# Layer 4 of a graph network: the 8-bit counts loaded nine pieces ahead, x and the own parts loaded through SP's queue

## The chip, the cores and the metric

The kernel runs on one core of a Trainium2 chip. The metric is the device time of one execution in microseconds; the time before is 2769.23 us, the median of three runs (2764.82 to 2772.06).

The engines are called as in the profile: PE (matrix products) with PEld (its weight loads), DVE (VectorE), ACT (ScalarE), POOL (GpSimd) and SP (SyncE, which only issues transfers). A transfer is issued by an engine, in that engine's order of instructions, so an instruction that waits holds back the transfers behind it.

## The reference

A graph of 6250 nodes with 256 features and 100000 edges (src to dst, sorted by dst) passes through four layers, and the result is added to x:

```python
h = jnp.maximum(_layernorm(x, axis=-1), 0.0)
h = _sage_mean(features, edge_src, edge_dst, n, deg, W1_self, W1_neigh, b1)
h = _sage_pool(h, edge_src, edge_dst, n, deg, W2_pool, b2_pool, W2_self, W2_neigh, b2)
h = _sage_gcn(h, edge_src, edge_dst, n, deg, W3_neigh, b3)
h = _sage_mean(h, edge_src, edge_dst, n, deg, W4_self, W4_neigh, b4)
return h @ W_fc + b_fc        # and x + this
```

Layer 4 is `h @ W_self + mean(h[src] over the edges of each node) @ W_neigh + b`. The kernel multiplies by the weights before it sums: what is left for the last stage is, for each node, the mean over its edges of rows of a table, plus an own part and x.

## The kernel before, in words

Nodes lie in 49 tiles of 128. Since dst is skewed to low numbers, a layer treats its first tiles (22 in layer 4, `H4`) as dense and the rest as sparse.

**Dense tiles.** `dense` (L569) forms, for one tile of targets, the sum over all 49 tiles of sources of a 128x128 matrix of edge counts times the sources' rows `zt` (128x512, the 256 features split into two halves): 22 x 49 = 1078 products into the PSUM bank `pd`. The counts are a table of 8-bit numbers in HBM (`tab_a`). `stream` (L1731) brings them: `load` (L1734) issues pieces of up to seven count tiles on ACT's queue (`nc.scalar`, L1742) into five buffers `ac`, four pieces ahead of the products; `widened` (L1750) turns a piece into 32-bit numbers `af` on ACT, three pieces ahead. Both are called at a piece's first product.

**Sparse tiles.** `sums` fetches 128 edges at a time: POOL gathers the rows of their sources into a ring of 14 slots (L495, 266 gathers in layer 4), DVE makes a one-hot matrix from the edges' targets (L491, six ahead), PE multiplies both into `pg` (L513), four gathers to a bank, and DVE adds `pg` to the sums `acc` (L545 the first, L547 the others). `Hub.advance` puts the dense products between the gathers, about four to each. The gathers, the products and the sums are issued in one order in the program; each engine then runs its own part of it in that order.

**Finishing a tile.** For each of the 49 tiles `load4` loads x into a buffer `xr4` (L1848) and the own part, left in HBM by layer 3, into `q4` (L1850); there are seven buffers of each, 128 KB each, and both loads are on ACT's queue. `finish4` adds the own part to x (L1864), then the sums times 1/degree (L1866; twice for a dense tile, once for each half of `pd`, as for the sparse `acc`), both on DVE, and stores the tile on SP's queue (L1869, called out). The instructions stand where the framework's scheduler puts them: it moves a load, and the addition at L1864, forward as soon as a buffer is free by its own reckoning. A load into an `xr4` buffer waits for the store of the tile that held it, a load into a `q4` buffer for DVE's L1864 of the tile that held it. Each transfer of SP and ACT counts up one of eight completion counters (DMAHW0 to 7), with one transfer under way on each.

**Source tiles.** 23 of the 49 tiles of `zt` are kept in SBUF from layer 3 (`z4_kept`, L1784); the other 26 (`z4_late`) are loaded from HBM at the start of layer 4 in four transfers on SP's queue (`resident`, L1774). The first 2 x 23 = 46 products use only kept tiles. Layer 4's first count pieces are loaded when its buffers open, at the start of layer 3 (about 1955 us), where ACT issues them; that layer's sums have a `stream` of their own (L1831).

Of the kernel before, what the change touches and what calls it, by code (L numbers as in the profile page):

```python
# [12 lines left out]
F8 = mybir.dt.float8e4  # L13
# [8 lines left out]
P = 128  # L22
# [57 lines left out]
def fast_path(  # L80
# [15 lines left out]
    nc = tc.nc  # L96
# [1631 lines left out]

    upto2.close()

    def stream(pool, chunks, wide_pool=None):  # L1731

        got = {}
        where = {(d, s): i for i, (d, s0, s1) in enumerate(chunks) for s in range(s0, s1)}  # L1734

        def load(i):
            if i >= len(chunks):
                return
            d, s0, s1 = chunks[i]
            got[i] = pool.tile([P, 7, P], F8, name="ac", bufs=5)  # L1740
            t = got[i][:, : s1 - s0, :]
            nc.scalar.dma_start(t.bitcast(BF16), tab_a[d, :, s0:s1, :])  # L1742

        wide = {}

        def widened(i):
            if i < len(chunks):
                n = chunks[i][2] - chunks[i][1]
                wide[i] = wide_pool.tile([P, 7, P], F32R, name="af", bufs=5)
                nc.scalar.copy(wide[i][:, :n, :], got[i][:, :n, :])  # L1750

        for i in range(4):
            load(i)
        if wide_pool:
            widened(0)
            widened(1)
            widened(2)

        def block(d, s):
            i = where[d, s]  # L1760
            if s == chunks[i][1]:
                if wide_pool:
                    widened(i + 3)
                load(i + 4)
            return (wide if wide_pool else got)[i][:, s - chunks[i][1], :]

        return block
# [10 lines left out]
    with ExitStack() as on:  # L1778
        psd = on.enter_context(tc.tile_pool(name="psd3", bufs=2, space=PSUM))
        psg = on.enter_context(tc.tile_pool(name="psg3", bufs=3, space=PSUM))  # L1780
        psm = on.enter_context(tc.tile_pool(name="psm3", bufs=2, space=PSUM))
        zk = on.enter_context(tc.tile_pool(name="fz4", bufs=1, side="right"))
        Z4 = {}
        z4_kept = ((20, 27), (27, 34), (34, 41), (41, 43))  # L1784
        z4_late = ((0, 7), (7, 14), (14, 20), (43, NT))
        for s0, s1 in z4_kept:
            zt = zk.tile([P, s1 - s0, 2 * FO], F32R, name=f"zt{s0}", bufs=1)
            Z4.update({s: zt[:, s - s0, :] for s in range(s0, s1)})

        with tc.tile_pool(name="fl3", bufs=2) as wk:  # L1790
            def done3(d, acc):
                q = wk.tile([P, FH], F32, name="q", bufs=2)
                if d < H3:
                    nc.vector.tensor_add(q, acc, acc3[d])
                    nc.vector.scalar_tensor_tensor(q, q, rgcn[:, d : d + 1], qrow,
                                                   op0=ALU.mult, op1=ALU.add)
                else:
                    if d in Z3:
                        z = Z3[d]
                    else:  # L1800
                        z = wk.tile([P, 3 * FH], BF16, name="zown", bufs=1)
                        with tc.issue_after(kept_stores[-1].ins):
                            nc.sync.dma_start(z, tab_r[d * P : (d + 1) * P, :])
                        yield 1
                        yield 1
                        yield 1
                    if d < NT - 4:
                        for part in range(3):
                            nc.vector.tensor_add(acc, acc, z[:, part * FH : (part + 1) * FH])
                            yield 1  # L1810
                    else:
                        own = bank(psm, "pm", "pm_own")
                        for part in range(3):
                            nc.tensor.matmul(own, ident_b, z[:, part * FH : (part + 1) * FH],
                                             start=(part == 0), stop=(part == 2))
                        yield 1
                        nc.vector.tensor_add(acc, acc, own)
                    nc.vector.scalar_tensor_tensor(q, acc, rgcn[:, d : d + 1], qrow,
                                                   op0=ALU.mult, op1=ALU.add)
                q2 = Z4[d] if d in Z4 else wk.tile([P, 2 * FO], F32R, name="q2")  # L1820
                halves(q[:, FO:], FO, q2)
                nc.sync.dma_start(tab_s[d * P : (d + 1) * P, :], q2.bitcast(F32))
                nc.sync.dma_start(xq[d * P : (d + 1) * P, :], q[:, :FO])
                yield 1

            late = ((0, 5), (5, KEPT), (EARLY[1], NT))
            Z3 = {s: kept_rows[:, s, :] for s in range(KEPT)}
            with tc.issue_after(kept_stores[-1].ins):
                for s0, s1 in late[2:]:
                    Z3.update(resident(wk, tab_r, FH, s0, s1))  # L1830
            block = stream(wk, [(d, s0, s1) for d in range(H3) for s0, s1 in late])  # L1831
            todo = []
            work = []
            for d in range(H3):
                work += dense([s for s0, s1 in late for s in range(s0, s1)], lambda s, d=d: block(d, s), lambda s: Z3[s], FH, psd,
                              lambda acc, d=d: todo.append(done3(d, acc)), own=d)
            sums(wk, psg, tab_r, FH, srcE, keyE, jb, H3, done3, 11, Hub(work), wait=14, todo=todo,
                 rest=12)

        upto3.close()  # L1840
        settle(zk, on.enter_context(tc.tile_pool(name="flp", bufs=1, space=PSUM)))
        with tc.tile_pool(name="fl4", bufs=2) as wk:
            loaded4 = {}

            def load4(d):
                n = P if d < NFULL else NREM
                xr = wk.tile([P, FI], F32, name="xr4", bufs=7)
                nc.scalar.dma_start(xr[:n, :], x[d * P : d * P + n, :])  # L1848
                q = wk.tile([P, FO], F32, name="q4", bufs=7)
                nc.scalar.dma_start(q[:n, :], xq[d * P : d * P + n, :])  # L1850
                loaded4[d] = n, xr, q

            def done4(d, acc):
                for i in (d, d + 1) if H4 <= d < NT - 1 else (d,):
                    if i not in loaded4:
                        load4(i)
                return finish4(d, acc)

            def finish4(d, acc):
                n, xr, q = loaded4.pop(d)  # L1860
                yield 1
                yield 1
                yield 1
                nc.vector.tensor_add(xr[:n, :], xr[:n, :], q[:n, :])  # L1864
                for c in range(0, acc.shape[1], FO):
                    nc.vector.scalar_tensor_tensor(xr[:n, :], acc[:n, c : c + FO],  # L1866
                                                   rmean[:n, d : d + 1], xr[:n, :],
                                                   op0=ALU.mult, op1=ALU.add)
                nc.sync.dma_start(out[d * P : d * P + n, :], xr[:n, :])  # L1869

            order = [*z4_kept, *z4_late]
            block = stream(zk, [(d, *c) for d in (0, 1) for c in z4_kept]
                           + [(d, *c) for d in (0, 1) for c in z4_late]
                           + [(d, *c) for d in range(2, H4) for c in order],
                           wk)
            todo = []
            parts4 = []
            for d in range(H4):
                parts4.append(dense([s for s0, s1 in order for s in range(s0, s1)],
                                    lambda s, d=d: block(d, s), lambda s: Z4[s], FO, psd,  # L1880
                                    lambda acc, d=d: todo.append(done4(d, acc)), wide=True))
            nk = sum(s1 - s0 for s0, s1 in z4_kept)
            hub = Hub([w for d in (0, 1) for w in parts4[d][:nk]]
                      + [w for d in (0, 1) for w in parts4[d][nk:]]
                      + [w for p in parts4[2:] for w in p])
            hub.advance(2 * nk)
            for s0, s1 in z4_late:
                Z4.update(resident(wk, tab_s, FO, s0, s1))
            sums(wk, psg, tab_s, FO, srcE, keyE, jb, H4, done4, 14, hub, wait=4, todo=todo,
                 rest=8, wide=True)  # L1890
# [643 lines left out]
```

## Time and profile before

| what | us |
| --- | --- |
| median of three runs | 2769.23 |
| the profiled execution, its own time | 2768.88 |
| its span, first to last instruction | 2767.1 |
| mean granted TensorE clock | 0.936 |
| layer 4's first product starts at | 2388.0 |
| last gather starts at | 2750.83 |

Over the whole span PE is busy 2363.3 us (85%), DVE 2074.8 (75%), POOL 1881.4 (68%) and ACT 1240.6 (45%). The page's share of busy time is an average over very different stages; what matters here is the last 380 us. A row of a group reads: line, engine, operation, output <- inputs, count | busy us, mean ns | idle time of the engine just before these, and what ended it. A row of the waits reads: engine, tile and line, what it waited for: us in total, times, the longest.

### The profile page before, as it was taken

The page shows a single profiled execution, that of the slowest core. Times are in us where ns is not written, and L with a number is a line of the kernel's source. Part 1 is how long each engine was busy: PE and PEld are TensorE (multiplying, and loading weights), DVE is VectorE, ACT ScalarE, POOL GpSimd, SP SyncE. Part 2 cuts the span into 40 slices and gives each one's busy share as a digit, 9 for nine tenths or more (in the row PEclk, how much of TensorE's full clock was granted, in tenths as well). Part 3 has the DMA queues.
Part 4 walks back from the last instruction along what each step waited for, and adds up shares of the span by engine and source line. Part 5 has one row for each costly group of instructions (what it writes and reads, how often), then busy time and mean ns, then how long its engine had stood idle before and what let it go on. Part 6 is the DMA issues. An engine that isn't in the chain of part 4 may idle for free.

```text
span 2767.1 us, 38367 instructions
## 1 busy us (share of the span) xinstructions
PE 2363.3 (85%) x10823; PEld 1341.6 (48%) x10913; DVE 2074.8 (75%) x5438; ACT 1240.6 (45%) x2833; POOL 1881.4 (68%) x2193
## 2 busy tenths in 40 slices
PE   3688999999686565788899998799899999798897
PEld 2356666767443222343344443344344444476676
DVE  8888777766699898788788897774376777466666
ACT  5467777763388887753444343211000000244333
POOL 5477777777566676777667776663477777577675
PEclk8799999999897687899999999999999999899999
DMA  8567777777799999999999999895799999999897
GB/s 273 154 183 204 208 210 212 223 228 222 243 362 334 309 351 318 331 347 345 315 307 331 342 357 298 296 311 189 280 370 382 379 391 388 328 344 308 284 302 225
DMA packets 360123, 815.18 MB, mean 295 GB/s; under 512 B 58798, under 2 KB 149014, under 8 KB 359868
## 3 DMA queue, kind: packets, MB, share of 16 engines
q0 software_dynamic: 145168, 511.30, 56.6%
q1 hardware_dynamic: 142248, 211.90, 21.1%
q10 hardware_dynamic: 72484, 89.43, 9.5%
q8 instruction: 89, 1.46, 0.2%
q14 instruction: 134, 1.10, 0.1%
HBM read 607.75 MB, written 205.46 MB: 294 GB/s over the span
## 4 chain that ended last, share of the span: by engine, by line
PE 45%; DMA 27%; DVE 14%; issue 5%; ACT 3%; POOL 2%; ACTq 0%; DVEq 0%; POOLq 0%
PE pd L575 14%; PE pg L516 11%; DMA X<-rows,srcIf 9%; DVE run L1631 5%; PE pd L569 4%; DMA ring<-tab_h,srcT 4%; DMA rows<-X 4%; PE pm_hp L1176 3%; DMA xr<-in_x 2%; DVE X L1631 2%; PE pm_prf L1548 2%; PE pm_hp L1170 2%; PE pb L346 2%; POOL X L1650 2%; DVE acc L547 1%
## 5 line engine op out<-in xcount | busy, mean ns | idle before, releaser
L1650 POOL DMA_INDIRECT X<-rows,srcIf x782 | 742.6, 950 | 346.6 <-issue 147.5
L1631 DVE SCALAR_TENSOR_TENSOR run<-run,samef,X 128x512 f32<-128x512 f32 x758 | 572.4, 755 | 65.3 <-DMA X<-rows,srcIf 59.6
L495 POOL DMA_INDIRECT ring<-tab_h,srcT x474 | 456.3, 963 | 148.9 <-issue 53.4
L516 PE MATMUL pg<-ring,hot 128*128 128x256 bf16 (+2 forms) x2342 | 492.1, 317 | 45.7 <-DMA ring<-tab_h,srcT 33.5
L575 PE MATMUL pd<-kept_rows,ae 128*128 128x512 bf16 x1520 | 395.0, 393 | 61.2 <-DVE acc L1307 48.2
L495 POOL DMA_INDIRECT ring<-tab_r,srcE x314 | 317.4, 1011 | 126.6 <-issue 49.4
L547 DVE SCALAR_TENSOR_TENSOR acc<-pg,M,acc 128x256 f32<-128x256 f32 (+2 forms) x629 | 322.8, 540 | 76.6 <-PE pg L516 72.5
L569 PE MATMUL pd<-zt,af 128*128 128x512 f32 x1078 | 305.8, 406 | 46.9 <-ACT af L1750 40.1
L516 PEld LDWEIGHTS <-hot 128*128 128x128 bf16 x2364 | 230.7, 98 | 233.2 <-issue 88.0
L495 POOL DMA_INDIRECT ring<-tab_s,srcE x266 | 254.4, 956 | 122.7 <-PE pg L513 48.7
L1631 DVE SCALAR_TENSOR_TENSOR X<-X,samef,run 128x512 f32<-128x512 f32 x379 | 282.2, 744 | 53.8 <-DMA X<-rows,srcIf 35.0
L575 PEld LDWEIGHTS <-ae 128*128 128x128 fp8e4 x1728 | 171.8, 100 | 305.3 <-issue 156.7
L569 PEld LDWEIGHTS pd<-zt,af 128*128 128x128 f32 x1078 | 208.0, 195 | 104.8 <-ACT af L1750 44.4
L1750 ACT CAST af<-ac 128x896 fp32r<-128x896 fp8e4 (+2 forms) x176 | 146.6, 846 | 217.5 <-PE pd L569 53.8
L491 DVE TENSOR_SCALAR hot<-iota_bf,keyE 128x128 bf16<-128x128 bf16 (+1 forms) x580 | 152.9, 284 | 107.8 <-PE pg L516 75.4
L1548 PE MATMUL pm_prf<-unf,hTf 128*128 128x512 f32 x384 | 197.4, 641 | 3.3 <-ACT hTf L1538 3.3
L401 ACT ACTIVATE A<-pb 128x392 fp8e4<-128x392 f32 x224 | 109.3, 499 | 191.2 <-PE pb L396 177.9
L338 ACT ACTIVATE hs<-ht,onef 128x128 bf16<-128x128 bf16 x396 | 153.5, 393 | 88.7 <-PE pb L346 87.7
L575 PE MATMUL pd<-Z,A 128*128 128x256 bf16 (+1 forms) x1176 | 184.6, 274 | 0.7 <-ACT A L351 0.6
L372 ACT ACTIVATE ht<-iota_bf,skR 128x128 bf16<-128x128 bf16 x448 | 155.9, 400 | 13.3 <-DMA col<-in_L_gnn_b 9.4
L337 ACT ACTIVATE ht<-iota_bf,sk 128x128 bf16<-128x128 bf16 x396 | 153.1, 398 | 8.3
L340 DVE TENSOR_SCALAR hm<-iota_w,mk 128x392 bf16<-128x392 f16 x461 | 150.5, 334 | 5.1 <-PE pb L346 4.8
(378 smaller groups left out, 3794.5 us busy)
## 6 DMA issues: line engine op xcount, KB each, us to landing
rows<-X SPq DMA_DIRECT2D x385, 256.0 KB
tab_r<-kept_rows ACTq DMA_DIRECT2D x44, 384.0 KB
ac<-tab_a ACTq DMA_DIRECT2D x128, 112.0 KB
rows<-hpf SPq DMA_DIRECT2D x49, 256.0 KB
th<-tab_t ACTq DMA_DIRECT2D x49, 256.0 KB
X<-rows,srcIf POOLq DMA_INDIRECT x782
tab_a<-A ACTq DMA_DIRECT2D x14, 784.0 KB
tab_t<-th SPq DMA_DIRECT2D x37, 256.0 KB
```

The lines of the kernel that those rows point to most:

```text
L337: nc.scalar.activation(t, iota_b, AF.Abs, bias=sk[:, r : r + 1])
L338: nc.scalar.activation(hots[0], t, AF.Relu, bias=one, scale=-1.0)
L372: nc.scalar.activation(held["ht"][:, i, :], iota_b, AF.Abs, bias=sk[:, r : r + 1])
L491: nc.vector.tensor_scalar(hot[j], iota_b, keyT[:, j - jb : j - jb + 1], None, op0=ALU.is_equal)
L495: nc.gpsimd.indirect_dma_start(out=ring[:, j % deep, :].bitcast(F32) if wide else ring[:, j % deep, :], out_offset=None, in_=table, in_off ...
L516: mm = nc.tensor.matmul(pg[:, : F + c], hot[j], X[:, part * F : (part + 1) * F + c], start=(k == 0 and part == 2), stop=(k == n - 1 and pa ...
L547: nc.vector.scalar_tensor_tensor(acc[d], half, m, acc[d], op0=ALU.mult, op1=ALU.add)
L569: nc.tensor.matmul(hold[0], a, z, start=(s == ss[0]), stop=(s == ss[-1]))
L575: nc.tensor.matmul(hold[0][:, : F + c], a, z[:, part * F : (part + 1) * F + c], start=(s == ss[0] and part == 2 and s != own), stop=(s == ...
L1548: nc.tensor.matmul(pm, hT[:, c, :], un[:, c, :], start=False, stop=(c == KH - 1))
L1631: nc.vector.scalar_tensor_tensor(put, held, st, row, op0=ALU.mult, op1=ALU.max)
L1650: nc.gpsimd.indirect_dma_start(out=X[:, k, :], out_offset=None, in_=tab_p, in_offset=bass.IndirectOffsetOnAxis(ap=srcI[:, t : t + 1], axis=0),
```

## The change

The stream of counts takes a parameter `deep` (4 unless given), and layer 4 gives 9: nine pieces are loaded ahead, in ten buffers instead of five. To make room, two source tiles less are kept (21), and 28 are loaded late, in five transfers; so the first products are 42. The loads of x and of the own parts go from ACT's queue to SP's. Layer 3's stream stays at four; the seven buffers of `xr4` and `q4` stay.

```diff
-    def stream(pool, chunks, wide_pool=None):
+    def stream(pool, chunks, wide_pool=None, deep=4):
...
-            got[i] = pool.tile([P, 7, P], F8, name="ac", bufs=5)
+            got[i] = pool.tile([P, 7, P], F8, name="ac", bufs=deep + 1)
...
-        for i in range(4):
+        for i in range(deep):
             load(i)
...
-                load(i + 4)
+                load(i + deep)
...
-        z4_kept = ((20, 27), (27, 34), (34, 41), (41, 43))
-        z4_late = ((0, 7), (7, 14), (14, 20), (43, NT))
+        z4_kept = ((22, 29), (29, 36), (36, 43))
+        z4_late = ((0, 7), (7, 14), (14, 18), (18, 22), (43, NT))
...
                 xr = wk.tile([P, FI], F32, name="xr4", bufs=7)
-                nc.scalar.dma_start(xr[:n, :], x[d * P : d * P + n, :])
+                nc.sync.dma_start(xr[:n, :], x[d * P : d * P + n, :])
                 q = wk.tile([P, FO], F32, name="q4", bufs=7)
-                nc.scalar.dma_start(q[:n, :], xq[d * P : d * P + n, :])
+                nc.sync.dma_start(q[:n, :], xq[d * P : d * P + n, :])
...
-                           wk)
+                           wk, deep=9)
```

The scheduler orders the instructions anew. ACT, in the second half of layer 4, has this before (casts are the widening; each load of x, of an own part and of counts in one line):

```order
L1742 DMA ac_26464<-tab_a_69 128x448 [waits DMAHW7_49,Activation_49]
L1848 DMA xr4_26760<-in_x 128x256 [waits DMAHW6_49,DMAHW0_49,DVE_49]
L1750 CAST af_26410<-ac_26393 128x768 [waits PE_49]
L1742 DMA ac_26478<-tab_a_69 128x128 [waits DMAHW2_49,Activation_49]
L1750 CAST af_26416<-ac_26412 128x768 [waits PE_49]
L1750 CAST af_26443<-ac_26418 128x896 [waits DMAHW3_49,PE_49]
L1742 DMA ac_26513<-tab_a_69 128x448 [waits Activation_49]
L1742 DMA ac_26532<-tab_a_69 128x448 [waits DMAHW4_49,Activation_49]
L1750 CAST af_26462<-ac_26445 128x896 [waits DMAHW5_49,PE_49]
L1848 DMA xr4_26835<-in_x 128x256 [waits DMAHW1_49,DVE_49]
L1742 DMA ac_26555<-tab_a_69 128x384 [waits Activation_49]
L1850 DMA q4_27305<-xq_70 128x256 [waits DMAHW7_49,DVE_49]
```

After the change only the casts and the count loads are left there. The loads of x and own parts stand on SP, between the stores, which were alone there before; around the same tiles (out_0 is the store):

```order
L1869 DMA out_0<-xr4_26349 128x256 [waits DMAHW3_49,DVE_49]
L1848 DMA xr4_26767<-in_x 128x256 [waits DMAHW6_49,DMAHW3_49]
L1869 DMA out_0<-xr4_26218 128x256 [waits DMAHW7_49,DVE_49]
L1850 DMA q4_27317<-xq_70 128x256 [waits DMAHW1_49,DVE_49]
L1848 DMA xr4_26848<-in_x 128x256 [waits DMAHW7_49,DMAHW2_49]
L1850 DMA q4_27346<-xq_70 128x256 [waits DMAHW5_49,DVE_49]
L1869 DMA out_0<-xr4_26381 128x256 [waits DVE_49]
L1848 DMA xr4_26930<-in_x 128x256 [waits DMAHW7_49,DMAHW3_49]
L1869 DMA out_0<-xr4_26519 128x256 [waits DMAHW4_49,DVE_49]
```

An x load there waits for the store in its buffer (the counter DMAHW7 of the second store, for xr4_26848) and holds the store after it; the own-part loads wait for DVE.

DVE, at the same tiles, before: the L1866 that finishes the tile in a buffer (xr4_26212) and, further down, the L1864 that reads the next x in that buffer (xr4_26835; a new number is a new tile in one of the seven buffers):

```order
L1866 SCALAR_TENSOR_TENSOR xr4_26212<-acc_26105,rmeanf_124,xr4_26212 128x256 [waits DVE_49]
...
L491 TENSOR_SCALAR hot_26502<-iota_bf_105,keyE_10813 128x128 [waits PE_49]
L491 TENSOR_SCALAR hot_26519<-iota_bf_105,keyE_10813 128x128 [waits PE_49]
...
L1866 SCALAR_TENSOR_TENSOR xr4_26375<-acc_26218,rmeanf_124,xr4_26375 128x256 [waits DVE_49]
...
L1866 SCALAR_TENSOR_TENSOR xr4_26506<-pd_26340,rmeanf_124,xr4_26506 128x256
L1864 TENSOR_TENSOR xr4_26835<-xr4_26835,q4_26837 128x256 [waits DMAHW5_49,DMAHW1_49]
L547 SCALAR_TENSOR_TENSOR acc_26381<-pg_26492,M_121,acc_26381 128x256 [waits PE_49]
```

And after the change, where the same buffer's tiles are called xr4_26218 and xr4_26848:

```order
L1866 SCALAR_TENSOR_TENSOR xr4_26218<-acc_26111,rmeanf_124,xr4_26218 128x256 [waits DVE_49]
...
L491 TENSOR_SCALAR hot_26513<-iota_bf_105,keyE_10813 128x128 [waits PE_49]
L1864 TENSOR_TENSOR xr4_26848<-xr4_26848,q4_26850 128x256 [waits DMAHW7_49,DMAHW2_49]
L491 TENSOR_SCALAR hot_26530<-iota_bf_105,keyE_10813 128x128 [waits PE_49]
...
L1866 SCALAR_TENSOR_TENSOR xr4_26381<-acc_26224,rmeanf_124,xr4_26381 128x256 [waits DVE_49]
```

Between the two rows that share a buffer stand 27 rows of DVE before and 14 after: the L1864 has moved up by 13.

## The prediction

> **What bounds the kernel now.** I read the windows of the last stage first, then its groups of instructions, its waits and the chain of waits. The change touches only layer 4 (2387 to 2767 us) and the loads that layer 3 starts ahead for it. The rows of the windows give, for each stretch, the busy time of each engine with its count of instructions, then the granted clock, the DMA share and the rate:
>
> ```profile
> 2412.00:2424.00 12.00, 4.58 (x11) 3.44 (x12) 0.91 (x3) 2.56 (x3) 2.48 (x3) 0.64 1.05 378
> 2430.00:2500.00 70.00, 69.48 (x303) 56.60 (x303) 46.55 (x143) 29.99 (x36) 53.07 (x56) 1.00 0.99 340
> 2500.00:2600.00 100.00, 90.31 (x380) 70.07 (x378) 63.98 (x200) 41.01 (x49) 75.25 (x79) 1.00 0.95 311
> 2600.00:2630.00 30.00, 23.80 (x86) 18.27 (x87) 15.98 (x50) 12.26 (x15) 16.69 (x18) 0.89 0.81 243
> 2630.00:2700.00 70.00, 65.63 (x274) 51.87 (x273) 41.05 (x130) 27.78 (x34) 50.68 (x53) 0.98 0.93 302
> 2700.00:2761.00 61.00, 52.15 (x216) 41.90 (x214) 44.06 (x131) 21.50 (x26) 34.40 (x36) 0.94 0.77 243
> ```
>
> From 2430 to 2500 POOL starts 56 gathers in 70 us, one each 1.25 us, and PE is busy throughout: this is the stage's best pace. Later it is missed. At 1.25 us each, the 79, 18, 53 and 36 gathers of the other rows would need 98.8, 22.5, 66.3 and 45.0 us; they had 100, 30, 70 and (the last gather starts at 2750.83) about 51. So about **18 to 20 us** are lost after 2500, and that is all this stage can win there. The groups and the waits say who loses it:
>
> ```profile
> L495 POOL DMA_INDIRECT ring<-tab_s,srcE x266 | 254.4, 956 | 122.7 <-PE pg L513 48.7 <-issue 33.5 <-PE pd L569 25.5
> L1864 DVE TENSOR_TENSOR xr<-xr,q 128x256 f32<-128x256 f32 (+1 forms) x49 | 20.7, 424 | 124.0 <-DMA xr<-in_x 99.1 <-DMA q<-xq 16.7 <-DMA ac<-tab_a 7.3
> ```
> ```profile
> DVE xr L1864 <- DMA xr<-in_x: 99.1, 27, 5.7
> PE pd L569 <- ACT af L1750: 25.9, 21, 5.1
> ACT af L1750 <- DMA ac<-tab_a: 22.3, 9, 4.2
> ACT af L1750 <- DMA xr<-in_x: 12.2, 3, 5.6
> DVE xr L1864 <- DMA q<-xq: 7.9, 5, 2.7
> ACT af L1750 <- DMA out<-xr: 7.6, 2, 7.2
> DVE xr L1864 <- DMA ac<-tab_a: 7.3, 1, 7.3
> ACT af L1750 <- DVE xr L1866: 7.1, 2, 5.1
> DVE acc L547 <- PE pg L513: 2.2, 4, 0.8
> DVE xr L1864 <- issue: 1.0, 1, 1.0
> DVE xr L1866 <- PE pd L569: 0.9, 1, 0.9
> ```
>
> The second fence holds the waits from 2430 on (total, times, longest). DVE waits 99.1 + 7.9 + 7.3 + 1.0 = **115.3 us** at one line, the addition of a tile's own part to its x (L1864), and only about 3 us for PE. The busy DVE times of the windows above add up to 212 us; 212 + 115 + 3 = 330 of the 331 us to 2761. DVE is thus always either at work or waiting for x. PE's 25.9 us behind ACT's widening are real, but beside a DVE that has no slack. The chain of waits from 2490 to 2720 shows why x is late (start, length, what):
>
> ```profile
> 2564.38 3.07 DMA out<-xr
> 2596.67 4.07 DMA out<-xr
> 2600.80 4.19 DMA xr<-in_x
> 2605.08 0.42 DVE xr L1864
> 2606.10 0.79 DVE acc L547 x2
> 2607.30 3.88 DMA out<-xr
> 2611.25 4.20 DMA xr<-in_x
> 2615.54 0.43 DVE xr L1864
> 2616.98 4.34 DMA out<-xr
> 2621.39 3.59 DMA xr<-in_x
> 2630.99 0.42 DVE hot L491 x2
> 2660.28 3.40 DMA xr<-in_x
> 2665.08 4.68 DMA out<-xr
> 2682.42 5.35 DMA xr<-in_x
> 2704.19 2.16 DMA out<-xr
> ```
>
> It is a **loop**: all seven x buffers are always taken, so a buffer's finished tile is stored (out), only then is the next x loaded into it, and DVE, in order, stands at L1864 until it lands. The eight stores of the chain before 2700 take 3.07 to 4.68 us, 4.13 on average; its sixteen loads of x 3.40 to 5.35, 4.24 on average. Round trip: about 8.3 us. In the three pairs shown around 2600 to 2621 the load leaves 0.06 to 0.07 us after the store lands, so there ACT's queue is not what makes it late.
>
> **The change, part by part.** *Both moved loads.* Bytes and buffers (seven) stay, so the loop stays. What the order of the two programs changes is how much DVE has to do inside it. I counted DVE's rows from the second half of a tile's L1866 (which lets its store go) to the L1864 that reads the next x in that buffer. Before: 17.8 rows on average (43 tiles); after: 13.7 (42 tiles), because several L1864 moved up, one of them 13 rows in the section above. Back to back, a sum takes 0.39 us and a one-hot row 0.21 (the rows at 2606.10 and 2630.99 are two each), about 0.32 per row in this mix: 5.7 us of work before, 4.4 after. If the round trip is L, each tile waits for L minus its own work, where that is positive. Added up tile by tile:
>
> - L = 8.3: 130 us before, 164 after
> - L = 8.0: 152 after
> - L = 7.5: 131 after
> - L = 7.0: 110 after
> - L = 6.5: 89 after
>
> The 130 stands against 115 measured, so I scale by 115/130 = 0.89. After: 146, 135, 116, 98 and 79 us. Against 115.3 that is +30, **+19**, +1, -18 and -36. Each microsecond of round trip is worth about 37 us, and the break-even lies at 7.5.
>
> What L will be is not in the trace. The nearest row for an x on SP's queue is the store, which has the same 128 KB, already goes through SP and shares that queue with no count pieces: 4.13 against x's 4.24. That alone gives 8.26 and +29. Against it: a stage that is slower by some 6% asks less of the DMA engines, and where the share was 0.77 a store took 2.16; where it was 0.81 (2600 to 2630) stores and loads still took 3.6 to 4.3. I take 8.0, near the store's row, and keep 6.5 and 8.4 for the range.
>
> A rule bears on this. The Trainium skill, "DMA: Bandwidth & Descriptors", section "Queues, rings and completion order", says that SP and ACT each have one row of rings on the same 16 engines, and that an engine takes turns between rows packet by packet. By it, an x on SP's row no longer stands behind a count piece in ACT's, so L could fall, to 7.0 say, and the sum would come out at -18 instead of +19. The trace speaks against it so far: the store has a row without pieces and takes 4.13 us all the same. That result is the first rival below.
>
> *SP's queue.* In the new order an x load stands behind the store it waits for and ahead of the next tile's store; own-part loads, which wait for DVE's L1864, stand in between. Each holds what is behind it. If the next store is due within those 4.1 us, it leaves late. Priced from nothing (stores lie a tile apart) to +5 us (one microsecond for a handful of them); I take 0 since 8.0 was taken from single round trips, and keep +5 for the range.
>
> *ACT's side.* x and own parts leave ACT, so the widening no longer stands behind a load that waits: 12.2 + 7.6 + 7.1 = 27 us of ACT's idle time go, and with nine pieces ahead most of the 22.3 us for counts. PE's 25.9 us go with them. I cost this at nothing: DVE at L1864 covers it, and is late next. If that cover were gone, it is worth the 18 to 20 us of gathers, not more.
>
> *Two more late source tiles.* The late tiles bind the stage's start:
>
> ```profile
>   DMA zt<-tab_s: 6.7, 1
> zt<-tab_s SPq DMA_DIRECT2D x2, 1792.0 KB
> zt<-tab_s SPq DMA_DIRECT2D x2, 1536.0 KB
> ```
>
> From 2412 to 2424 PE has 4.58 us of work in 12 at a DMA share of 1.05; it waits for source tiles. Two more of 256 KB are 0.52 MB, at the 378 GB/s of that row 1.4 us; four fewer first products (46 to 42) do not matter, since PE waits anyway. Gathers share that rate, so the cost is 0.5 to 2 us: I take **+1**. Deeper counts buy nothing there, for they are not what is late.
>
> *Layer 3's end of the prefetch.* Nine pieces and one more are loaded at the start of layer 3 instead of four and one, 0.5 MB more, beside this wait:
>
> ```profile
> 1955.00:1969.00 14.00, 6.46 (x28) 2.91 (x29) 0.63 (x5) 0.58 (x1) 6.61 (x7) 0.87 0.94 324
> 1968.46 1.44 PE L516 MATMUL pg<-ring,hot 128*128 128x512 bf16 x3 [7.05 <-DMA ring<-tab_r,srcE]
> ```
>
> 0.5 MB at 324 GB/s is 1.5 us if all of it comes ahead of the first gathers, nothing if behind: **+0.7**.
>
> *Sum.* 2768.88 (the profiled run) + 19 + 1 + 0.7 = 2789.6. The median of the runs is 0.35 higher: **2790 us**.
>
> **Rivals.** *Faster.* Without the count pieces beside it, x lands sooner, L falls below 7.3, and DVE's waits shrink by up to 36 us. Then ACT's and PE's gains show too, and POOL's pace decides: 18 to 20 us won, 1 to 2 given up at the start, 2769 - 18 = **2751**. For it: 5.35 us for an x where 3.40 is possible. Against it: the store's 4.13 us, and the DMA share of 0.93 to 0.99 wherever POOL keeps pace; a faster stage asks for more, not less. It decides from L = 7.3 down.
>
> *No change.* L near 7.5: the wait that goes at ACT comes back at L1864: **2770**. Also here: the change doesn't do what it says, since count loads share completion counters with SP's stores and loads and may be held behind them, so that nine ahead becomes five. ACT then waits as now, and DVE too.
>
> *Slower still.* L = 8.4 and SP's queue in full: +32 + 5 + 2 = **2808**.
>
> **How the numbers follow.** Forecast and "slower still" (L from 7.8 to 8.4): 0.58; no change: 0.13; faster: 0.29. Runs of this kernel can tell some 0.3% (8 us) from no change, so these are also the chances of slower, same and faster. The range goes from 2750, the middle of the faster rival, to 2808, since less than that would leave out more than 2 in 10; the forecast's own range is 2778 to 2808.
>
> **What would show it.** Right: DVE's wait for x at L1864 grows from 99 to about 120 to 130 us, while PE's wait for the widening and ACT's for loads nearly go; the chain of waits still alternates store, x, L1864; round trips stay near 8. Wrong: x loads of 3 us or less, gathers 1.25 us apart to the end, DVE waiting for PE's sums instead; or a first stretch to 2430 that grows by more than 2 us. What would make the prediction wrong is above all the tally: it takes each tile's wait alone, though a wait at one L1864 lets the next x come in.

## The result, and the profile after

The changed kernel takes 2795.47 us (median of four runs, 2787.85 to 2798.97) against 2769.53 before: 25.9 us longer, ratio 1.0092 (95% interval 1.0067 to 1.0117). The forecast was 2790.

The profiled run took 2787.85 us, the lowest of the four, with a span of 2786.0. In it layer 4's first gather starts at 2381.22, 6.7 us earlier than before; layer 3's first gather was already 7.5 us earlier (1952.76 against 1960.28), ahead of everything that the change touches. From layer 4's first gather to the end of the span the change takes 2786.0 - 2381.22 = 404.8 us against 2767.1 - 2387.92 = 379.2: **25.6 us longer**, nearly the whole difference of the medians (25.9). From layer 3's first gather to layer 4's it is 428.5 against 427.6.

The windows of the last stage in the changed kernel (columns as in the prediction: PE, PEld, DVE, ACT and POOL busy, granted clock, DMA share, GB/s):

```profile
2430.00:2500.00 70.00, 63.94 (x274) 50.85 (x273) 41.02 (x128) 29.14 (x35) 50.73 (x53) 1.00 0.96 321
2500.00:2600.00 100.00, 84.37 (x342) 66.44 (x341) 59.88 (x187) 36.90 (x44) 63.20 (x66) 0.95 0.85 267
2600.00:2630.00 30.00, 23.63 (x90) 17.93 (x89) 17.43 (x56) 11.46 (x14) 17.61 (x20) 0.89 0.85 269
2630.00:2700.00 70.00, 59.70 (x246) 46.45 (x245) 38.39 (x120) 25.27 (x30) 46.28 (x49) 0.97 0.88 279
```

From 2500 to 2600 there are 66 gathers where there were 79. Counted from the stage's first gather, the 81st stands at 112.2 us (before 111.0), the 101st at 147.7 (135.9), the 201st at 288.7 (271.5) and the last at 387.2 (362.9). So the start is nearly as before, and the loss collects from about the 85th gather on.

The groups from 2387 and the waits from 2430 on, in the changed kernel:

```profile
L1864 DVE TENSOR_TENSOR xr<-xr,q 128x256 f32<-128x256 f32 (+1 forms) x49 | 20.8, 427 | 144.0 <-DMA xr<-in_x 101.1 <-DMA ac<-tab_a 35.9 <-DMA q<-xq 7.1
```
```profile
DVE xr L1864 <- DMA xr<-in_x: 101.1, 33, 7.0
DVE xr L1864 <- DMA ac<-tab_a: 35.9, 8, 7.0
DVE xr L1864 <- DMA q<-xq: 3.7, 3, 2.0
PE pd L569 <- ACT af L1750: 3.6, 5, 0.9
ACT af L1750 <- DMA ac<-tab_a: 5.6, 2, 3.1
ACT af L1750 <- DMA q<-xq: 33.0, 12, 5.5
ACT af L1750 <- DMA out<-xr: 18.9, 9, 4.8
ACT af L1750 <- DMA xr<-in_x: 12.4, 9, 2.4
PE pg L513 <- issue: 36.9, 17, 5.0
```

DVE waits 101.1 + 35.9 + 3.7 = **140.7 us** at L1864 instead of 115.3, that is 25.4 more, and the stage is 25.6 longer. PE's wait for the widening has gone from 25.9 to 3.6 us, and ACT's for count pieces from 22.3 to 5.6, and nothing of it reached the end: PE now waits 36.9 us at the sparse products (L513), where it had no such wait before, for something that the profile doesn't name. Nor has ACT stopped waiting for x, own parts and stores: 33.0 + 18.9 + 12.4 = 64.3 us against 22.7 before (12.2 and 7.6 in the prediction's fence, and 2.9 for own parts). A count load takes over a completion counter from an earlier transfer, now often one of SP's, and holds ACT until that has landed; one at 2509.94 waited for the own part issued at 2504.98. PE hardly notices.

The 35.9 us "for counts" are not counts, which L1864 doesn't read: L1864 waits for two counters, and the piece named had taken over one of them and was on its way in the same moments. In the chain of waits x for the addition at 2549.42 is issued at 2545.21 and the piece at 2545.22. Read so, x accounts for 101.1 + 35.9 = 137.0 us, against 99.1 + 7.3 = 106.4 before. The chain, between 2490 and 2745:

```profile
2545.22 4.18 DMA ac<-tab_a
2549.42 0.47 DVE xr L1864
2549.91 0.32 SPq L1850
2550.32 4.61 DMA xr<-in_x
2555.02 0.42 DVE xr L1864
...
2558.81 3.82 DMA out<-xr
2562.64 0.33 SPq L1848
2563.07 5.05 DMA out<-xr
2568.18 4.83 DMA xr<-in_x
2573.04 0.43 DVE xr L1864
```

It is the loop of before, store, x, addition, with stores of 3.8 to 5.1 us and loads of 4.6 to 4.8 here. The SPq steps are new. At 2549.91 it is an own-part load, which waited for the addition at 2549.42 and kept the x load behind it 0.6 us longer than its own store did. At 2562.64 it is an x load. SP's own rows and DVE's show what it does (start, length, operation):

```profile
2558.81 0.34 SPq L1869 DMA_DIRECT2D out<-xr  x1
2562.64 0.33 SPq L1848 DMA_DIRECT2D xr<-in_x  x1
2563.07 0.38 SPq L1869 DMA_DIRECT2D out<-xr  x1
```
```profile
2560.07 0.48 DVE L1866 SCALAR_TENSOR_TENSOR xr<-acc,rmeanf,xr 128x256 f32<-128x256 f32 x1
```

DVE has finished a tile at 2560.55. Its store leaves at 2563.07, 2.5 us late, because on SP the x load ahead of it waits until 2562.64 for the store before.

I took these times for every tile whose x load waits for a store: end of the last L1866, issue of the store, issue of the x load into the same buffer, start of its L1864. Means over the tiles at which DVE then waits (before and the depth alone are without one tile each at the start of the stage, whose load stood 9.8 and 8.4 us on ACT's queue after the store had landed):

| | before | depth alone | queue alone | the change |
| --- | --- | --- | --- | --- |
| tiles with a wait over 0.3 us | 28 of 41 | 31 of 41 | 42 of 42 | 40 of 42 |
| L1866's end to the store's issue | 0.03 | 0.03 | 0.71 | 0.77 |
| store's issue to x's issue | 4.64 | 4.33 | 4.35 | 4.12 |
| x's issue to L1864 | 4.40 | 4.12 | 4.44 | 4.42 |
| sum | 9.07 | 8.48 | 9.50 | 9.30 |
| DVE's waits at L1864 from 2430 on | 115.3 | 124.7 | 142.6 | 140.7 |

(The two columns in the middle are the first experiments below.)

### The profile page after: what moved, and what is told of

It reads as the page before. It is cut to its first block, busy times and chain, and to the rows that moved or that the text cites. A ratio compares the mean times of both kernels' runs of the same rounds, so it can differ in the third digit from the quotient of the medians.

```text
span 2786.0 us, 38399 instructions
## 1 busy us (share of the span) xinstructions
PE 2371.6 (85%) x10823; PEld 1345.6 (48%) x10913; DVE 2073.4 (74%) x5438; ACT 1240.6 (45%) x2833; POOL 1880.5 (67%) x2193
## 4 chain that ended last, share of the span: by engine, by line
PE 39%; DMA 32%; DVE 14%; issue 5%; ACT 4%; POOL 3%; ACTq 0%; SPq 0%; DVEq 0%; POOLq 0%
PE pd L575 12%; PE pg L516 10%; DMA X<-rows,srcIf 9%; DVE run L1631 5%; DMA ring<-tab_h,srcT 4%; DMA out<-xr 4%; DMA xr<-in_x 4%; DMA rows<-X 3%; PE pm_hp L1176 3%; PE pm_w L274 2%; PE pm_hp L1170 2%; PE pm_prf L1548 2%; DMA ring<-tab_r,srcE 2%; PE pb L346 2%; DVE X L1631 2%
## 5 line engine op out<-in xcount | busy, mean ns | idle before, releaser
L491 DVE TENSOR_SCALAR hot<-iota_bf,keyT 128x128 bf16<-128x128 bf16 x474 | 124.3, 271 | 39.7 <-PE pg L516 38.9
```

What stands on the lines that cost most here:

```text
L491: nc.vector.tensor_scalar(hot[j], iota_b, keyT[:, j - jb : j - jb + 1], None, op0=ALU.is_equal)
```

## The experiments

**Theory A**, that of the prediction: DVE reads x too early. It stands at L1864 until the round trip of store and x load is over, and the new order puts fewer of its rows into that trip. **Theory B**: SP's queue, on which x and own-part loads now hold the stores behind them. **A third**: the depth and the two source tiles given up for it.

**The depth alone.** The change, with both loads on ACT's queue again:

```diff
-                nc.sync.dma_start(xr[:n, :], x[d * P : d * P + n, :])
+                nc.scalar.dma_start(xr[:n, :], x[d * P : d * P + n, :])
...
-                nc.sync.dma_start(q[:n, :], xq[d * P : d * P + n, :])
+                nc.scalar.dma_start(q[:n, :], xq[d * P : d * P + n, :])
```

> The change without the moved loads: nine pieces ahead, 21 kept source tiles, x and own parts still on ACT's queue. Theory A (the loss is DVE's place in the loop of store and x load: the new order puts L1864 nearer to the L1866 that frees its buffer): the tally by rows gives 15.1 rows on average and DVE waits of 144 us at a round trip of 8.3 us, a walk that lets waits overlap 130, so 15 to 29 us more than before's 115: 2785 to 2800 us. Theory B (the loss is SP's queue, where x loads and own-part loads hold the stores behind them): SP holds only stores here, so only the two late tiles and the prefetch are left, 2769 to 2772 us.

Measured: 2778.75 us, before 2770.31, ratio 1.0027 (1.0006 to 1.0048). That is some 8 us longer, and in neither theory's range: A had 2785 to 2800, B 2769 to 2772. Its waits from 2430 on:

```profile
DVE xr L1864 <- DMA xr<-in_x: 102.5, 28, 6.6
PE pd L569 <- ACT af L1750: 26.2, 21, 3.4
DVE xr L1864 <- DMA q<-xq: 16.3, 7, 4.7
DVE xr L1864 <- issue: 5.9, 2, 4.5
```

DVE waits 124.7 us, not 144: the rows are closer together as counted (14.8 on average in the trace, 17.5 before), but the trip is 0.6 us shorter, a thing I had not counted. And PE waits 26.2 us for the widening, as before with four pieces (25.9). So it was not for want of pieces that ACT was late for PE; the next two experiments show that it was the loads of x and of own parts in its own queue, and these only while DVE's early read keeps the buffers late.

**The queue alone.** The kernel before, both loads through `nc.sync`, four pieces, 23 kept tiles:

> The kernel before with x and own parts on SP's queue, four pieces ahead, 23 kept tiles. Theory A: 13.7 rows on average as in the change, DVE waits about 146 us: 2790 to 2800 us, that is the whole loss without depth. Theory B: the same time, 2790 to 2800. A third theory, that the depth and the two tiles given up cost it: 2769 us.

Measured: 2796.53 us, ratio 1.0098 (1.0074 to 1.0121): the whole loss, to which the depth adds nothing. DVE's waits, and PE's for the widening:

```profile
DVE xr L1864 <- DMA xr<-in_x: 110.8, 32, 6.0
DVE xr L1864 <- DMA ac<-tab_a: 23.1, 8, 4.0
DVE xr L1864 <- DMA q<-xq: 7.1, 3, 3.0
DVE xr L1864 <- issue: 1.6, 1, 1.6
PE pd L569 <- ACT af L1750: 1.7, 3, 1.1
```

PE's wait is gone here with four pieces ahead. The third theory falls: the loss is there without the depth. A and B both expected this time, so it doesn't part them.

**x added last, in the kernel before and in the change.** DVE adds the sums to the own part and x at the end, so that nothing reads x before the tile's sums are there:

```diff
-                nc.vector.tensor_add(xr[:n, :], xr[:n, :], q[:n, :])
                 for c in range(0, acc.shape[1], FO):
-                    nc.vector.scalar_tensor_tensor(xr[:n, :], acc[:n, c : c + FO],
-                                                   rmean[:n, d : d + 1], xr[:n, :],
+                    nc.vector.scalar_tensor_tensor(q[:n, :], acc[:n, c : c + FO],
+                                                   rmean[:n, d : d + 1], q[:n, :],
                                                    op0=ALU.mult, op1=ALU.add)
+                nc.vector.tensor_add(xr[:n, :], xr[:n, :], q[:n, :])
```

> The kernel before, with the sums added to the own part first and x added last, so that DVE reads x only once the tile's sums are there. The result is the same sum. Theory A: L1864's early place is what makes DVE wait; without it DVE's waits for x fall from 115 to under 15 us and the gathers keep 1.25 us apart but for ACT's late widening: 2750 to 2758 us. If instead the seven buffers or the DMA engines are too few for the pace whatever DVE's order, the wait stays over 60 us and the time near 2769.

> The changed kernel, with x added last in the same way. Theory A: DVE's waits for x fall from 141 to under 15 us, and with ACT's waits gone too the gathers keep 1.25 us apart: 2749 to 2755 us, no slower than the kernel before with the same edit. Theory B: SP's queue still holds the stores, buffers come free late, and it stays 15 us or more above the kernel before with the same edit.

Measured: 2750.17 us (ratio 0.9925, 0.9901 to 0.9949) and 2750.45 (0.9932, 0.9909 to 0.9956). Both are as theory A had it, and they are the fastest of the study. The addition is now in L1868. Its group in the kernel before with this edit, then in the change with it:

```profile
L1868 DVE TENSOR_TENSOR xr<-xr,q 128x256 f32<-128x256 f32 (+1 forms) x49 | 20.5, 418 | 0.2
```
```profile
L1868 DVE TENSOR_TENSOR xr<-xr,q 128x256 f32<-128x256 f32 (+1 forms) x49 | 20.5, 418 | 0.4
```

DVE's wait for x is gone. The windows of the change with x added last:

```profile
2430.00:2500.00 70.00, 70.00 (x307) 57.10 (x306) 50.72 (x151) 33.94 (x41) 52.02 (x56) 1.00 1.01 347
2500.00:2600.00 100.00, 98.98 (x429) 79.94 (x428) 77.29 (x227) 47.15 (x56) 75.94 (x80) 1.00 0.97 324
2600.00:2700.00 100.00, 95.13 (x402) 73.56 (x401) 70.00 (x206) 45.33 (x53) 75.92 (x80) 1.00 0.96 321
```

80 gathers in 100 us are one each 1.25 us, to 2700: POOL's pace, 0.95 us for a gather and 0.30 to the next, the closest that gathers come in any of these traces. PE is busy 95 to 100% there too, so it has little left either. x, own parts and stores all still go through SP here, with the same seven buffers, and the DMA share is 0.96 to 1.01. SP still holds stores: they leave 0.60 us late on average, 18 of the 49 by over 0.3 us and one by 6.1. But between the row that lets a buffer's store go and the one that reads its next x DVE now has 98 rows on average (13.7 in the change), and x has landed at least 23 us before it is read. So SP's queue, the buffers and the DMA engines all allow this pace; what did not was the place at which DVE reads x. B alone is not the cause: a late store costs only while DVE stands waiting for what comes behind it.

That the two are equal answers the question of the depth too. With DVE's wait gone, POOL's pace is next, and PE's waits from 2430 to 2740 list none for the widening in either kernel, though the kernel before has x and own parts still on ACT's queue, and four pieces. Nine pieces have nothing to add.

**Five more kernels, on two other chips.** These ran in three groups, each beside the kernel before: the first on a second chip, where the kernel before took 3190.73 us, the second on a third chip (3158.03), the third on the second chip again (3153.74). Layer 4's gathers came about 1.5 us apart there whatever the edit (the last one 392 to 400 us after the first). So the times tell nothing of the theories, and none of the times expected below, which are for the first chip, could be met. Only waits within one group can be set side by side.

*Half of each store* (the change with `out[..., : FI // 2]`; half of the output is left out):

> The changed kernel, storing only the first 128 of each row's 256 results (the other half of the output is left out). The order of DVE's and SP's rows is that of the change, row for row. Theory A (the wait is round trip minus DVE's work, added up over the tiles): each microsecond that store and x load get shorter together takes about 37 us from DVE's waits of 141. If the store falls by 0.8 us, the waits fall by about 30 us and the time to about 2766; if the store does not get shorter, nothing changes. A rival, that the loss is SP's order (x and own-part loads ahead of the stores) and not the length of the trip: waits fall by 10 us at most, 2785 or more.

> Once more, since the kernel before took 3191 us on the chip of that call: the changed kernel, storing only the first 128 of each row's 256 results (the other half of the output is left out); the order of rows is that of the change. Theory A: the round trip is what DVE waits out; if the store falls from 4.1 us by 0.8, DVE's waits of 141 us fall by some 30 and the kernel takes about 2766 us; each microsecond of round trip is worth 37 us. If the store is not shorter with half the bytes, the time stays at 2795. Rival (SP's order, not the length of the trip): waits fall by 10 us at most, 2785 or more although the store is shorter.

Measured: 3192.07 in the first group (ratio 1.0002, 0.9973 to 1.0031) and 3154.52 in the second (0.9991, 0.9963 to 1.0018).

*x through ACT's queue, own parts through SP's:*

> The changed kernel with x loaded through ACT's queue again, own parts through SP's. Theory A: the order of rows gives 13.3 rows and waits of 150 us by the tally, at an unchanged round trip: 2790 to 2800 us, as slow as the change. If x leaves ACT's queue as early as with the depth alone (round trip 0.55 us shorter than before), 129 us and 2782. Theory B (x loads standing before stores on SP are the loss): the stores now wait only behind own-part loads, 2772 to 2780.

> Once more for the same reason: the changed kernel with x loaded through ACT's queue, own parts through SP's. Theory A: 13.3 rows between a buffer's rows and waits of 150 us by the tally at an unchanged round trip, 129 at the shorter trip that the depth alone showed (8.5 us against 9.1): 2782 to 2800 us. Theory B (x loads standing before stores on SP are the loss): stores leave at once, 2772 to 2780.

> The changed kernel with x loaded through ACT's queue, own parts through SP's, a third time, after two calls on a chip where the kernel before took 3158 to 3191 us. Theory A: 2782 to 2800 us (13.3 rows; waits of 150 us by the tally at the trip of before, 129 at the shorter one that depth alone showed). Theory B (x loads standing before stores on SP are the loss): 2772 to 2780 us.

Measured: 3195.33 (1.0031, 1.0006 to 1.0055), 3155.64 (0.9984, 0.9965 to 1.0003) and 3156.59 (1.0018, 0.9988 to 1.0049) in the first, second and third group.

*x through SP's queue, own parts through ACT's:*

> The changed kernel with the own parts loaded through ACT's queue again, x through SP's. Theory A: 13.4 rows, waits of 149 us: 2793 to 2803 us. Theory B with the own-part loads as the ones that hold the stores: 2775 to 2782; with the x loads as those: 2795.

Measured: 3201.02 in the first group (1.0038, 1.0003 to 1.0073).

*Ten x buffers instead of seven* (`name="xr4", bufs=10`):

> The changed kernel with ten x buffers instead of seven. If the loop of store and x load is a matter of buffers alone, three more give 43% more time per tile and DVE's waits vanish: about 2750 us. Theory A: the scheduler moves L1864 forward as far as the new buffers allow, the rows between stay 13.5 on average, the tally gives 135 us against 146 for the change: 2783 to 2792 us.

Measured: 3188.31 in the first group (1.0011, 0.9985 to 1.0038).

*A store buffer of its own:*

```diff
                 for c in range(0, acc.shape[1], FO):
-                    nc.vector.scalar_tensor_tensor(xr[:n, :], acc[:n, c : c + FO],
+                    o = xr
+                    if c + FO == acc.shape[1]:
+                        o = wk.tile([P, FI], F32, name="o4", bufs=4)
+                    nc.vector.scalar_tensor_tensor(o[:n, :], acc[:n, c : c + FO],
...
-                nc.sync.dma_start(out[d * P : d * P + n, :], xr[:n, :])
+                nc.sync.dma_start(out[d * P : d * P + n, :], o[:n, :])
```

> The changed kernel, whose last L1866 of a tile writes to a buffer of its own (four of them) that is stored, so that an x buffer is free when DVE has read it and not when its store has landed. L1864 stays early. Theory A (DVE waits out store plus x load): the trip is the x load alone, about 4.4 us, and what is left are x loads that stand on SP behind a store due 8 to 14 rows of DVE earlier: 1 us or so for each tile, waits of 30 to 60 us instead of 141, which the 331 us of the stage can cover: 2750 to 2762 us. Rival (the queue that x shares, or the early L1864 whatever the trip): waits stay over 100 us, 2780 or more.

Measured: 3150.24 in the third group (0.9984, 0.9957 to 1.0012).

The groups of L1864 from the start of layer 4. First group: half stores, ten x buffers, x through SP's queue with own parts through ACT's, x through ACT's queue with own parts through SP's:

```profile
L1864 DVE TENSOR_TENSOR xr<-xr,q 128x256 f32<-128x256 f32 (+1 forms) x49 | 20.7, 425 | 99.5 <-DMA xr<-in_x 52.4 <-issue 27.8 <-DMA ac<-tab_a 15.3
L1864 DVE TENSOR_TENSOR xr<-xr,q 128x256 f32<-128x256 f32 (+1 forms) x49 | 20.5, 424 | 99.2 <-DMA xr<-in_x 44.0 <-issue 40.9 <-DMA q<-xq 11.6
L1864 DVE TENSOR_TENSOR xr<-xr,q 128x256 f32<-128x256 f32 (+1 forms) x49 | 20.7, 425 | 104.0 <-DMA xr<-in_x 65.4 <-issue 34.8 <-DMA ac<-tab_a 3.7
L1864 DVE TENSOR_TENSOR xr<-xr,q 128x256 f32<-128x256 f32 (+1 forms) x49 | 20.6, 423 | 82.9 <-DMA xr<-in_x 55.8 <-issue 21.3 <-DMA q<-xq 5.8
```

Second group: half stores, x through ACT's queue. Third group: x through ACT's queue, the store buffer:

```profile
L1864 DVE TENSOR_TENSOR xr<-xr,q 128x256 f32<-128x256 f32 (+1 forms) x49 | 20.8, 428 | 125.6 <-DMA xr<-in_x 60.4 <-issue 45.9 <-DMA ac<-tab_a 17.3
L1864 DVE TENSOR_TENSOR xr<-xr,q 128x256 f32<-128x256 f32 (+1 forms) x49 | 20.7, 425 | 100.7 <-DMA xr<-in_x 58.4 <-issue 35.7 <-DMA ac<-tab_a 4.0
```
```profile
L1864 DVE TENSOR_TENSOR xr<-xr,q 128x256 f32<-128x256 f32 (+1 forms) x49 | 20.8, 426 | 84.9 <-DMA xr<-in_x 57.5 <-issue 21.2 <-DMA q<-xq 6.2
L1864 DVE TENSOR_TENSOR xr<-xr,q 128x256 f32<-128x256 f32 (+1 forms) x49 | 20.1, 420 | 37.9 <-issue 16.6 <-DMA q<-xq 11.1 <-DMA xr<-in_x 10.2
```

With the store out of the loop DVE waits 37.9 us, within the 30 to 60 that theory A expected, though the time does not follow there. Three more buffers leave 99.2, the same as the half stores of that group (99.5): ten buffers instead of seven don't take the wait away, since L1864 moves forward with them (14 rows between the two that share a buffer). Half a store is hardly shorter: in the first group 3.92 us from its issue to the x load's, against 4.00 and 4.04 in the two other kernels that load x through SP. That experiment did not change the trip enough to test what a microsecond of it is worth, so the half stores stand for the change here, which itself did not run on these chips.

With x off SP DVE waits 17 us less than with half stores in the first group (82.9 against 99.5) and 25 less in the second (100.7 against 125.6), where the tally by rows expected no less (13.3 rows against 13.7). Stores leave 0.03 us after L1866 there instead of 0.65 to 0.68. With own parts off SP and x still on it nothing is gained: 104.0 us, and stores 0.64 us late. So on these chips it is the x loads on SP that hold stores, as one form of theory B had it, and that bears on the wait by more than the tally allows.

**What stays open.** How the 25 us share out between fewer rows in the trip and stores held on SP. Both come with the move, and both act through DVE's early read of x. An estimate, from the tally at the trips of the table: 159 us for the kernel before, 166 for the depth alone, 206 for the change. From the kernel before to the change the rows alone give 38 of the 48, since the trip is nearly as long. From the depth alone to the change, where the measured waits grow by 16 us, the rows give only 5 to 7 of the 40; the rest is the trip, and of its 0.82 us SP's hold is 0.74. The kernel that would part them, x through ACT's queue and own parts through SP's, with rows as few as the change's, never ran on the first chip.

## Why the prediction was right

*The bound.* Right. DVE without slack, its waits at L1864 were the stage: 25.4 us more wait, 25.6 us more time, and 0.2 to 0.4 us of wait, POOL's pace, when x is read last. By the labels of the waits, x took 137.0 us where 120 to 130 was named as the sign. The faster rival's 2751 was the right price for POOL's pace; the change just doesn't reach it, and 2750 needs an edit in another place.

*DVE's rows in the trip.* Right in direction and use. The traces have 13.7 rows instead of 17.5 (17.8 counted for before), and 40 of 42 tiles wait instead of 28 of 41. The tally overstates: at the trips that the table shows it gives 159 us before and 206 after, a growth by 1.30, and the waits grew by 140.7/115.3 = 1.22. It prices each tile alone, which the prediction named as its weak point.

*The round trip.* The mis-sized term. I took 8.0, below the 8.3 of before, because a slower stage asks less of the DMA engines. It did not fall: 9.30 against 9.07 where DVE waits, with a DMA share of 0.85 to 0.96 from 2430 to 2700. The 8.3 itself was too short for before, in part since the chain shows stores and loads but not the time for which some x loads stood on ACT after the store had landed (0.36 us on average, five of the 28 by over 0.3 us). That part did go with the move (4.64 to 4.12 us from store to x).

*Luck.* That 2790 came within 6 us of 2795 is in part luck, since two errors offset each other. With the measured trips, 9.07 and 9.30, the tally scaled to the 115.3 us of before as in the prediction gives 150 us after: +35 instead of the +19 forecast and the +25 measured. A trip taken too short hid how much the tally overstates.

*The rule on rows of rings.* By it x could have come sooner on SP's row. It did not: 4.42 us from issue to L1864 in the change and 4.44 in the queue alone, against 4.40 on ACT's row before and 4.12 in the depth alone.

*SP's queue.* I took 0 and kept +5. It holds stores by 0.77 us on average where DVE waits: 15 of those 40 by over 0.3 us, one by 4.0. That is more than the move won at ACT (0.52), so the trip did not shrink. At my own 37 us for each microsecond of trip 0.77 would be 28 us, so +5 was too small a bound.

*ACT's side, at nothing.* Right, and the cover was named: PE's 25.9 us became 3.6 and gave nothing. That nine pieces take part in it was wrong: depth alone leaves 26.2, the queue alone 1.7. The sign that ACT's waits for loads nearly go did not come: they grew to 64.3 us, through the shared counters that the prediction named under *No change*, but without any cost that PE shows.

*Two late tiles, +1, and layer 3, +0.7.* Too small to be seen. The 81st gather comes 1.2 us later, but over the six kernels of the first chip it lies between 109.3 and 114.2 us, and the queue alone, which gives up no tile, has 114.1. Layer 3's 427.6 and 428.5 us lie within 427.4 to 428.7 in the same way.

## What to carry to other kernels

When an engine works in order, look at where in its row it first reads a loaded value, before moving the load: a read that stands long before its result is needed makes the engine pay the whole trip, store and load. More buffers need not help (ten instead of seven left 99 us of wait), since a scheduler that moves the read forward as far as the buffers allow uses them up. Put the loaded operand into the last operation; here that saved 20 us in the kernel before (2770.31 to 2750.17) and 45 in the changed one (2795.47 to 2750.45). And before a prefetch is made deeper, check what the late engine is queued behind: here it was other loads on its own queue, not missing pieces.

## What the runs showed of the hardware

A 128 KB load of x took 4.1 to 4.4 us from issue to use in the four kernels of the table, on ACT's queue and on SP's alike, at DMA shares of 0.77 to 0.99 in the windows of the kernel before and the change; halving a store's bytes took about 0.1 us off the time from its issue to that of the x load waiting for it (3.92 against 4.00 and 4.04). A transfer that waits on SP holds those behind it: stores up to 4.0 us in the change, 6.1 with x added last. And chips differ: on the second and third the kernel before took 3153.74 to 3190.73 us instead of 2770.31; there DVE shows 17 to 46 us of waits at L1864 that end in nothing the profile shows, against 1.0 in the kernel before on the first. Why was not tried.
